# Expert weights kept in SBUF, and expert results scattered into two planes in token order, in a fused attention and mixture-of-experts kernel

## The chip, the cores and the metric

The kernel runs on one core of one Trainium2 chip, in one launch. The time is device microseconds (us) of one execution. A second source is the profile, which is one execution recorded by the hardware profiler: PE is TensorE's matmuls, PEld its weight loads, DVE is VectorE, ACT is ScalarE, POOL is GpSimd, and SP is the engine that only issues transfers. A name such as L1298 is a line of the kernel before.

## What is computed

The input has 8 items (B) of 256 channels and 32 x 32 positions, so 1024 tokens of 256 values each. Everything is float32. Layer 0 is attention with 8 heads of 64, whose softmax runs over the queries, with a projection and a residual. Layer 1 is attention of the normalised tokens with themselves, and then a mixture of 8 experts of which each token uses two:

```python
# layer 0, per item: xt is (S, C)
q, k, v = split(xt @ w_qkv + b_qkv)
attn = softmax(q k^T * SCALE, axis=queries)
t = attn v @ w_out + b_out + xt
# layer 1
a = ln(t); t = t + softmax((a W^T) a^T) a
n = ln(t)
probs = softmax(n @ router_w.T)
rw, re = top_k(probs, 2); rw = rw / rw.sum(-1)
out = n
for e in range(8):
    h = gelu(n @ w1[e] + b1[e])
    out = out + combine[:, e] * (h @ w2[e] + b2[e])
t = t + out        # and back to channels first
```

## The kernel before, in words

The items are worked through in turn. For each item `layer0` runs 32 steps of a head pair g and a key block j: `score` (L493) puts the products of keys and queries into PSUM, two passes on VectorE find the maximum (L508, L517), ScalarE takes the exponential (L534), and `gather_values` (L570) accumulates the result. Then `pr` (L672) projects, and `attend` does the attention of layer 1: `pt` transposes (L281), `px` (L709), score products `ps` in a scheme with seven products (L772), exponentials, transposes of the weights by VectorE, SP transfers and ScalarE copies (`turn`, L861), and eight `mix` steps (`py`, L878; the sum on VectorE at L887). `normed` normalises and turns the result, and `logits` makes the routing scores. In items 0 to 6 `attend` and `normed` call `Begin.at` at named places, and this puts projections and values of the next item (`pqk`, L349, and `pv`, L408) between the steps. In the layer 0 of items 1 to 7, `gather_values` uses empty instructions on SP (`relay.nop()`) to hold an order on TensorE.

The experts are done in two ways. Items 0 to 6 form one group. `dispatch` counts how many tokens go to each expert, gives every choice of a token a row, and scatters normalised tokens into `rows` in DRAM (L1110, two scatters for each of 8 token blocks, from POOL). During layer 0 of item 7, `plan` works out which expert each of 63 blocks of 256 rows belongs to. After layer 0 of item 7, `experts` runs over the 63 blocks in a pipeline written out in its last loop. `fetch` loads a block's rows with four transfers from an address that SP reads from SBUF into a register (L1276, L1281). `weights` has POOL gather 128 rows of 1282 floats, the two weight matrices and both biases, from `wpack` in DRAM (L1264) into one of four buffers `wb`; the gather is skipped by an index out of bounds where the buffer already holds this expert. `turned` transposes on VectorE (L1287), `hidden` multiplies (`ph`, L1298) and applies the gelu on ScalarE (L1308), and `collect` multiplies again (`pe`, L1324), adds the second bias on VectorE (L1334) and has POOL write the block to `y` in DRAM (L1341), in block order. `places` works out meanwhile on VectorE where in `y` each token's two results stand. `wpack` is written at the very start, behind the zero fill of `rows` (L295), by `pack` (L313 to L327).

`Results` then gathers for every block of 128 tokens the two result rows of each token (`yk`, L1420, on POOL), and adds them, times the gate, to the token's sum (L1442, on VectorE). A table of places, `PLACES`, spreads these gathers, adds and stores over the attention of item 7 and over the dense stage. The dense stage, `dense`, does the experts of item 7 without sorting: for each expert and half of the tokens, four products of 512 columns with two weight tiles (`pdh`, L1547), the gelu (L1556), the second product (`pdy`, L1571), and the gated sum (L1580). Its weights come by 16 transfers on SP into three of the `wb` buffers. `store` transposes (L1478) and writes to the output (L1485).

The order on each engine is mostly that of the program, held in places by `tc.issue_after` and `tc.add_manual_dep`.

## Time and profile before

| what | us |
|---|---|
| median of 3 runs (lowest, highest) | 2335.08 (2328.76, 2335.84) |
| profiled execution, its time | 2330.56 |
| profiled execution, span of the core | 2328.6 |
| TensorE busy | 2258.4 (97% of the span) |
| VectorE busy | 1556.0 (67%) |
| ScalarE busy | 1171.3 (50%) |
| GpSimd busy | 409.0 (18%) |
| last `pr` of item 7 to the end of the expert blocks | 1856.9 to 2097.4 |
| attention of item 7, norm and turn | 2097.4 to 2194.4 |
| dense stage | 2194.4 to 2321.3 |

A row of a group gives the line, the engine, the operation, what is written and read with shapes, the count, then busy time and the mean in nanoseconds, and after the second bar the idle time of the engine just before it with what ended it. A row of a stage gives its limits, its length, and for each engine the busy time and the number of instructions, then the granted TensorE clock, the share of time that the 16 DMA engines were busy, and GB/s. A busy TensorE is not a TensorE at its peak; four pairs of a weight load and a matmul of 256 columns follow each other at 1.73 us in the expert stage, though each matmul is listed with 0.38.

### The profile page before, as it was taken

How to read it: one execution, taken by the hardware profiler on the slowest of the kernel's cores; microseconds unless marked ns; L12 is line 12 of the kernel's file. 1: busy time of each engine (PE TensorE's matmuls, PEld its weight loads, DVE VectorE, ACT ScalarE, POOL GpSimd, SP SyncE). 2: the span in 40 equal slices, each digit the busy share in tenths (PEclk: the TensorE clock that was granted, in tenths of full speed). 3: DMA queues.
4: the chain of work that ended last, by engine and by line, in shares of the span. 5: the costliest groups of instructions: out<-in, count | busy, mean ns of one | idle time of the engine just before them, and what ended most of it. 6: DMA issues, size and time to landing. Idle time of an engine off the chain costs nothing.

```text
span 2328.6 us, 37960 instructions
## 1 busy us (share of the span) xinstructions
PE 2258.4 (97%) x13059; PEld 1217.2 (52%) x13059; DVE 1556.0 (67%) x4029; ACT 1171.3 (50%) x2154; POOL 409.0 (18%) x392
## 2 busy tenths in 40 slices
PE   9999999999999999999999999999999999998798
PEld 3344633563456335633564355435553488884565
DVE  5775678557865786578657775777668766436655
ACT  3664466356635663656465647465646622225211
POOL 0000012000200030003000200020002135545553
PEclk9999999999999999999999999999999999999899
DMA  8995201020103010201020101100111156675554
GB/s 293 385 386 153 68 15 42 5 58 10 47 1 63 6 51 1 44 19 53 3 45 19 49 8 28 35 26 13 22 41 42 50 144 191 192 202 141 160 180 136
DMA packets 274407, 199.57 MB, mean 86 GB/s; under 512 B 185224, under 2 KB 227880, under 8 KB 272424
## 3 DMA queue, kind: packets, MB, share of 16 engines
q1 hardware_dynamic: 248120, 138.62, 21.2%
q0 software_dynamic: 25008, 58.01, 7.7%
q8 instruction: 104, 1.70, 0.3%
q10 hardware_dynamic: 1088, 0.52, 0.1%
q14 instruction: 87, 0.71, 0.1%
HBM read 108.88 MB, written 110.90 MB: 94 GB/s over the span
## 4 chain that ended last, share of the span: by engine, by line
PE 81%; ACT 5%; DVE 4%; DMA 3%; issue 3%; SPq 2%; POOL 1%; another core or an unknown queue 1%; DVEq 0%; ACTq 0%; POOLq 0%
PE po L570 19%; PE psc L493 19%; PE pqk L371 7%; PE py L878 6%; PE pr L672 5%; PE pv L408 4%; PE ph L1298 3%; PE pe L1324 3%; PE ps L772 3%; PE pdh L1547 2%; PE pdy L1571 2%; PE px L709 2%; PE pqk L349 2%; SPq L861 2%; PE ps1z L772 1%
## 5 line engine op out<-in xcount | busy, mean ns | idle before, releaser
L534 ACT ACTIVATE ex<-psc,nmax 128x1024 f32<-128x1024 f32 x512 | 570.0, 1114 | 300.1 <-DVE scrap L517 217.9
L493 PE MATMUL psc<-qk,qk 64*64 64x512 f32 x4096 | 575.9, 592 | 3.9 <-ACT ex L534 3.6
L570 PE MATMUL po<-ex,vs 64*64 64x512 f32 x4096 | 570.7, 591 | 3.6 <-DVE vs L550 2.6
L517 DVE TENSOR_SCALAR_CACHE_REDUCE scrap<-psc,nmax 128x512 f32<-128x512 f32 x512 | 384.5, 751 | 159.9 <-PE psc L493 131.9
L508 DVE TENSOR_REDUCE nmax<-psc 128x1 f32<-128x512 f32 x512 | 350.5, 685 | 9.3 <-PE psc L493 9.3
L493 PEld LDWEIGHTS psc<-qk,qk 64*64 64x64 f32 x4096 | 180.4, 132 | 279.3 <-ACT ex L534 132.8
L570 PEld LDWEIGHTS po<-ex,vs 64*64 64x64 f32 x4096 | 176.5, 132 | 275.5 <-DVE vs L550 82.2
L1110 POOL DMA_INDIRECT rows<-n,d_at x112 | 109.0, 973 | 661.2 <-DVE nmax L508 660.9
L1037 POOL TENSOR_TENSOR t<-t,n 128x2048 f32<-128x2048 f32 x8 | 36.3, 4534 | 875.3 <-DVE n L263 875.3
L371 PE MATMUL pqk<-xT,wqkv 128*128 128x512 f32 x384 | 171.2, 599 | 0.0
L336 ACT ACTIVATE qk<-pqk,b_qks 128x512 f32<-128x512 f32 x124 | 85.6, 690 | 86.6 <-PE pqk L371 77.5
L878 PE MATMUL py<-n,spare 128*128 128x256 f32 x512 | 120.2, 391 | 5.1 <-DMA out_dram<-oT 3.3
L1420 POOL DMA_INDIRECT yk<-y,yat x112 | 109.7, 979 | 79.5 <-issue 28.8
L408 PE MATMUL pv<-wqkv,xT 128*128 128x512 f32 x256 | 121.4, 599 | 2.2 <-ACT wqkv L120 1.2
L371 PEld LDWEIGHTS pqk<-xT,wqkv 128*128 128x128 f32 x384 | 71.0, 190 | 99.9 <-issue 76.8
L861 ACT COPY spare<-home 32x256 f32<-32x256 f32 x272 | 109.4, 402 | 15.5 <-DVE home L849 10.5
L878 PEld LDWEIGHTS py<-n,spare 128*128 128x128 f32 x512 | 99.3, 196 | 28.2 <-issue 11.6
L672 PE MATMUL pr<-wo,res 128*128 128x256 f32 x512 | 111.9, 379 | 0.7 <-ACT res L589 0.7
L672 PEld LDWEIGHTS pr<-wo,res 128*128 128x128 f32 x512 | 97.2, 190 | 17.7 <-ACT res L589 4.7
L1308 ACT ACTIVATE hb<-ph,wb 128x256 f32<-128x256 f32 x96 | 40.1, 470 | 127.4 <-issue 86.6
L534 ACT ACTIVATION_READ_ACCUMULATOR ex<-psc,nmax 128x1 f32 x512 | 99.1, 194 | 0.0
L887 DVE SCALAR_TENSOR_TENSOR t<-py,rs,t 128x256 f32<-128x256 f32 x64 | 30.5, 477 | 98.4 <-PE py L878 85.9
(256 smaller groups left out, 2943.3 us busy)
## 6 DMA issues: line engine op xcount, KB each, us to landing
rows<-wb SPq DMA_DIRECT2D x7, 8192.0 KB
xr<-rows SPq DMA_DIRECT2D x252, 64.0 KB
y<-yb POOLq DMA_DIRECT2D x63, 256.0 KB
xs<-in_x_dram SPq DMA_DIRECT2D x64, 128.0 KB
spare<-home SPq DMA_DIRECT2D x240, 32.0 KB
out_dram<-oT SPq DMA_DIRECT2D x60, 128.0 KB
xT<-in_x_dram SPq DMA_DIRECT2D x7, 1024.0 KB
sums<-t SPq DMA_DIRECT2D x7, 1024.0 KB
```

Of the source, the lines that this page charges most:

```text
L371: mm = nc.tensor.matmul(pq[:, ts(n, 512)], wqkv[:, cc, t, ts(g, P)], xT[:, cc, ts(n, 512)], start=(cc == 0), stop=(cc == NCC - 1),)
L408: nc.tensor.matmul(pv, self.xT[:, cc, ts(i, P)], wqkv[:, cc, 2, :], start=(cc == 0), stop=(cc == NCC - 1),)
L493: mm = nc.tensor.matmul(pss[at, h][ts(c, DK), ts(n, 512)], k[r, j * P + c * DK : j * P + (c + 1) * DK], q[r, ts(n, 512)], start=True, stop ...
L508: firsts[at, h] = nc.vector.tensor_reduce(nmax, pss[at, h][:, ts(0, 512)], AX.X, ALU.max, negate=True)
L517: seconds[h] = nc.vector.tensor_scalar(scrap, pss[at, h][:, ts(1, 512)], -1.0, nmaxes[at, h], ALU.mult, ALU.min, accum_out=nmax,)
L534: nc.scalar.activation(ex, pss.pop((at, h)), AF.Exp, bias=nmaxes.pop((at, h)), scale=1.0, accum_out=sums[at][:, h : h + 1],)
L570: mm = nc.tensor.matmul(po[n][ts(h, DK), :], vss[at][keys, h, :], exps[at, h][keys, ts(n, 512)], start=(j == 0 and turn == 0), stop=(j == ...
L672: nc.tensor.matmul(pr[:, :C], res[:, g, ts(i, P)], wo[:, g, :], start=(g == 0), stop=(g == NPAIR - 1))
L861: move(to[ts(k, SQ), a], since[ts(a, SQ), k])
L878: evicted["mixed"] = nc.tensor.matmul(py[:, :D], aT[m], n1[:, m, :], start=(m == 0), stop=(m == NT - 1))
L1110: scatter = nc.gpsimd.indirect_dma_start(out=view[:, :], out_offset=bass.IndirectOffsetOnAxis(ap=ats[k][:, i : i + 1], axis=0), in_=n2[:, ...
L1420: ins = nc.gpsimd.indirect_dma_start(out=self.slot(at)[:, k, :], out_offset=None, in_=self.group.y[:, :], in_offset=bass.IndirectOffsetOnAxis(
```

## The change

At the start of item 7, `keep_experts` loads both weight matrices of all 8 experts into one tile in SBUF, 32 KB in each partition; `pack`, `wpack` and the `wb` buffers go. In the expert stage ScalarE copies the 1024 columns of a block's expert out of the table into a ring of four buffers (`stage`), from an address in a register. The addresses are read from SBUF into registers in lists of 16 blocks: for SP (the rows), ScalarE (weights, and first bias) and VectorE (second bias). The skipping of blocks that share an expert goes: each block has its copy.

Each row of `rows` has two values more, the gate and the place of its result (counted from the end, so that zero means none); POOL writes them beside the normalised tokens before each set of scatters. In `experts` they come by a fifth transfer. `collect` multiplies by the gate, converts the place to an integer, and POOL scatters the 256 result rows by two indirect transfers into `y`, which now has two planes in token order. `places` goes. The products of the last four blocks are put later: `fill` calls their second products in `attend` ("between", "between 2") and in "norm 2", and the first products of the last two at "last weights".

`Results` begins only after item 7 is normed. It loads half items with three direct transfers (the sum and two planes) into five slots, adds twice and stores, one half item at each of the dense steps. `dense` reads weights straight from the table. Since the table has its channels in the order of the 32 x 32 transposes, item 7's norm writes its channels in that order (`squares=True`), the routing uses a router matrix in that order (`rTs`), and the sum of t and n on POOL becomes four instructions. Some tiles change places (layer 0's `res` of item 7, `mixes`).

```diff
-    WROW = NCC * FF + NFC * D + NFC + D
-    NWB = 3
-    NXB = NWB + 1
+    WE = NCC * FF + NFC * D
+    WAYS = 16
+    NXB = 4
+    LATE = 4
+    DW = D + 2
...
+    def keep_experts():
+        table = one.tile([P, E, WE], F32, tag="res", name="table")
+        src = w1.rearrange("e (k cc c) f -> k cc c e f", k=NQ, c=SQ)
+        for k in range(NQ):
+            for cc in range(NCC):
+                nc.sync.dma_start(table[ts(k, SQ), :, ts(cc, FF)], src[k, cc])
+        at = NCC * FF
+        for fc in range(NFC):
+            nc.sync.dma_start(
+                table[:, :, at + fc * D : at + (fc + 1) * D],
+                w2.rearrange("e (fc p) d -> fc p e d", p=P)[fc],
+            )
+        return table
...
-    def pack():
...
+            self.rows = dram.tile([E * self.cap + BR, DW], F32, name=f"rows_{n}")
-            self.y = dram.tile([self.nb * BR, D], F32, name=f"y_{n}")
+            self.y = dram.tile([2 * self.cap, D], F32, name=f"y_{n}")
+            self.planes = self.y.rearrange("(k n p i) d -> n p k i d", k=2, p=P, i=NT)
...
         for k in range(2):
             for i in range(NT):
                 behind = yield
-                view = group.views[2 * (NT * group.items.index(b) + i) + k]
+                if i == 0:
+                    nc.gpsimd.tensor_copy(n2[:, :, D], gate[:, k, :])
+                    nc.gpsimd.iota(
+                        n2[:, :, D + 1],
+                        [[-1, NT]],
+                        base=2 * group.cap - (k * len(group.items) + which) * S,
+                        channel_multiplier=-NT,
...
-    def places(group):
...
+        def register(b, which):
+            if (b, which) not in held:
+                some = min(WAYS, group.nb - b)
+                engine, top = KINDS[which]
+                _, values = nc.values_load_multi_w_load_instructions(
+                    group.where[which][0:1, b : b + some],
+                    engines=[engine],
...
+            return held[b, which]
+
+        ring = one.tile([P, NXB, WE], F32, tag="v", name="w_ring")
+        spare = two.tile([P, LATE // 2, WE], F32, tag="xT", name="w_late")
...
+        def stage(b):
+            late = b - (group.nb - LATE // 2)
+            wb = ring[:, b % NXB] if late < 0 else spare[:, late]
+            firsts[b], seconds[b] = wb[:, :W1], wb[:, W1:]
+            some = W1 if -LATE // 2 <= late < 0 else WE
+            nc.scalar.copy(wb[:, :some], flat[:, bass.ds(register(b, 1), some)])
...
-        def weights(b):
-            wb = wbs_x[b % NXB]
-            nc.gpsimd.indirect_dma_start(
...
+            loads.append(
+                nc.sync.dma_start(
+                    where, group.rows[bass.ds(at, BR), D:].rearrange("(r p) c -> p r c", r=R)
+                )
+            )
...
-                    bias=wb[:, at + fc : at + fc + 1],
+                    bias=b1T[:, bass.ds(at + fc, 1)],
...
-                    wb[:, at : at + D].unsqueeze(1).to_broadcast([P, R, D]),
-                )
+                    b2_flat[:, bass.ds(register(b, 3), D)].unsqueeze(1).to_broadcast([P, R, D]),
+                )
+                where = wheres.pop(b)
+                nc.vector.tensor_mul(yb, yb, where[:, :, 0:1].to_broadcast([P, R, D]))
+                to = small.tile([P, R], I32, tag="to", name=f"to_{n}_{b}", bufs=4)
+                nc.vector.tensor_scalar(
+                    to, where[:, :, 1], -1.0, float(2 * group.cap), ALU.mult, ALU.add
+                )
-            nc.gpsimd.dma_start(group.y[ts(b, BR), :].rearrange("(r p) d -> p r d", r=R), yb)
+            for r in range(R):
+                nc.gpsimd.indirect_dma_start(
+                    out=group.ways[R * b + r][:, :],
+                    out_offset=bass.IndirectOffsetOnAxis(ap=to[:, r : r + 1], axis=0),
+                    in_=yb[:, r, :],
...
         for b in range(group.nb + 4):
-            if b - 3 in rows:
+            if b - 3 in rows and b - 3 < group.nb - LATE // 2:
                 hiddens[b - 3], last = hidden(b - 3, rows.pop(b - 3))
+            if 0 <= b - 1 < group.nb:
+                stage(b - 1)
             if b < group.nb:
                 rows[b] = fetch(b)
...
     class Results:
-        SLOTS = 8
-        PLACES = {
...
+            self.sent += 1
+            nc.sync.dma_start(self.totals[at], self.group.sums[n][:, ts(h, NB), :])
             for k in range(2):
+                nc.sync.dma_start(
+                    self.slots[at][:, k], self.group.planes[n][:, k, ts(h, NB), :]
+                )
...
+        def add(self, behind):
...
+            with tc.issue_after(behind.ins):
+                for k in range(2):
+                    nc.vector.tensor_add(total, total, self.slots[at][:, k])
...
+        def tick(self, k, behind):
+            if self.stored < self.added:
+                self.store()
+            if self.added < len(self.todo):
+                self.add(behind)
...
-            if n == NH2 - 1 and e + NWB < E:
-                weights(e + NWB)
...
+        if b == B - 1:
+            table = keep_experts()
...
-        experts(groups[0], evicted["divided"])
-        others = Results(groups[0])
-        others.begin()
+        product, result = experts(groups[0], evicted["divided"], table)
...
+            if place == "between":
+                result(end - 4)
+            elif place == "between 2":
+                result(end - 3)
+            elif place == "last weights":
+                product(end - 2)
+                product(end - 1)
+            elif place == "norm 2":
+                with tc.issue_after(evicted["mixed"].ins):
+                    result(end - 2)
+                    result(end - 1)
```

## The prediction

> **What bounds the kernel now.** I read the busy row by slice first, then busy time by stage, then waits, then the chain that ended last.
>
> ```profile
> PE   9999999999999999999999999999999999998798
> PEclk9999999999999999999999999999999999999899
> POOL 0000012000200030003000200020002135545553
> ```
> TensorE is full, and in full clock, until the last tenth. Only the end, where GpSimd is busy too, has holes. Stages, with PE, PEld, DVE, ACT, POOL, clock, DMA share, GB/s:
>
> ```profile
> 1870.75:2097.40 226.65, 220.78 (x1009) 190.22 (x1008) 112.30 (x291) 54.16 (x128) 107.66 (x120) 1.00 0.67 185
> 2099.76:2181.55 81.79, 68.81 (x216) 42.84 (x216) 52.02 (x119) 41.64 (x91) 46.91 (x48) 0.92 0.60 162
> 2181.55:2194.35 12.80, 4.98 (x25) 2.85 (x24) 11.66 (x30) 0.41 (x2) 6.37 (x5) 0.83 0.74 218
> 2194.35:2321.30 126.95, 120.75 (x422) 77.82 (x418) 72.64 (x170) 24.30 (x37) 60.88 (x61) 0.96 0.49 146
> 1635.15:1702.84 67.69, 64.93 (x225) 40.43 (x224) 35.79 (x85) 41.43 (x91) 0.00 (x0) 1.00 0.23 39
> ```
> They are: the expert blocks; item 7's attention from px to its last mix; from there to the dense stage; the dense stage; and, last, item 6's attention over the same steps as item 7's. Item 6 needs 14.1 us less although it also does two value products (3.4 us) for an item that follows: its VectorE has 16 us less to do, and its clock is 1.00 against 0.92. So item 7's attention is held up by the gathering and adding put into it.
>
> ```profile
> L1442 DVE SCALAR_TENSOR_TENSOR o<-yk,gate,o 128x256 f32<-128x256 f32 x44 | 18.4, 476 | 0.0
> L1420 POOL DMA_INDIRECT yk<-y,yat x52 | 50.7, 975 | 36.3 <-issue 12.5 <-DVE t L887 10.7 <-DVE o L1442 5.0
> PE ph L1298 <- DMA wb<-wpack,w_at: 4.5, 6, 1.2
> PE py L878 <- DMA out_dram<-oT: 3.3, 1, 3.3
> ```
> The first two rows cover that attention stage; the last two are waits of TensorE. In the expert stage the chain itself leaves TensorE again and again for a y store and then weights, here at 1914 us (start, us, what).
>
> ```profile
> 1914.06 4.22 DMA y<-yb
> 1918.29 2.90 issue
> 1921.18 5.71 DMA wb<-wpack,w_at
> 1927.03 1.97 PE ph L1298 x8
> ```
>
> **The change, part by part.** The sum is against the profiled execution (2330.56 us, span 2328.6); the median of the runs, 2335.08, is 4.5 above it, and I carry the difference over to the median.
>
> *Start.* Packing the weights goes (SP busy with it 153 to 212 us, after the zero fill). In item 0 the steps px to last mix take 72.6 us (189.50 to 262.14), in item 1 66.8 (435.59 to 502.36): 5.8 us lost while this traffic drains. The fill stays, with rows 0.8% longer. Taken: -4.5; ends -6 and +2 (odd row lengths might write slower; no row shows it).
>
> *Expert stage.* A block is 1.727 us for ph and 1.727 for pe; 63 make 217.6, the stage takes 226.65, so stalls are 9. Four pe and two ph halves, 6 x 1.727 = 10.4, move to later. What stays: 120 x 1.727 + 0.4 at the start = 207.6, or -19.0 before new waits. The new work per 3.45 us block:
> - ACT: gelus 0.84 a pair, plus a copy of 128x1024. Nearest rows: exp over 128x1024 in SBUF 1.15, 128x512 copy 0.585, 32x256 copy 0.402, so 0.95 to 1.15; I take 1.1. With address arithmetic (SP's own, 0.05 to 0.15) about 2.2: covered by the wait for ph.
> - DVE: transpose 0.70, add 0.69, the new gate product (same shape) 0.69, the index conversion 0.15: 2.2. The `places` work goes. Covered.
> - POOL: two indirect scatters at 0.97 to 1.03 (rows of the scatters and of the weight gathers) against 1.03 + 0.77 now: 2.1, covered. yb has two buffers, 6.9 us; 1.5 (DVE) + 2.1 + some 2.5 to land is 6.1. If landing takes 4.2, as the chain shows with weights in the way, DVE waits 1 us, and the two PSUM buffers hide it.
> - SP: a fifth DMA per block, 256 short pieces, 0.32 to 0.65: 2.7 of 3.45; fetches run 3 blocks ahead.
> - Register loads, in lists of 16: ACT two lists, DVE and SP one, every 16 blocks. This is the one part that nothing covers. The row:
>
> ```profile
> L1276 SPq TENSOR_LOAD <-row_at x63: 263/276/1116, 1856.3 to 2074.8; - x63
> ```
> At 0.276 a list is 4.4 us in which its engine starts nothing else. Behind the list of weight addresses stands the copy for block 16 (ready at 7.3 us, PE wants it at 6.9: 0.4 late); behind that of the bias addresses stands the gelu of block 16, 1.2 late, for which pe waits; behind DVE's stands the next xb transpose, 1.2 late. That is 2.8 us, three times, and some 2 at the start, where the first bias list may sit behind item 7's square root at 1872.8. Together 10. The Trainium skill ("DMA: Bandwidth & Descriptors", Latency and other measured facts) speaks against the change: a floor of about 0.6 us per `tensor_load`. A list is then 9.6 us, copy and gelu are 5.6 and 7.2 late, 38 for three groups, with start and DVE 44 to 55: an estimate, and the whole gain. I go by the row, whose 63 loads are of the same kind on another engine. Ends: 2 (lists hoisted or overlapped) and 55. Taken: -19.0 + 10 = -9.0.
>
> *Item 7's attention.* Gathers, 44 adds, five transposes for stores and the weight loads leave. Item 6 is the model: 67.7, less its own filling (3.4), plus two pe and two ph halves (6.9) = 71.2, against 81.8: -10.6. Ends -14 and 0: the results bring DVE 1.5 us each, and two gelu pairs bring ACT 1.7 plus a table load of 1.28 and perhaps one back. Cover is the slack that item 6 shows; if it is gone, each comes whole.
>
> *Last mix to dense.* Now 12.8: the norm of seven blocks runs after adds and transposes on DVE. Then: the norm of the last block 2.5, beside two pe halves (3.45); DVE work on their results 3.0, then nT copies of 1.22 each, 8.7 together: -4.1. The add of t and n on POOL becomes four instructions with 32-element runs, 4.5 to 9 us (now 4.53 in one), behind two result scatters: done 14 to 17 us after the last mix; the first dense add wants it at 19.
>
> *Dense.* TensorE's own work is 16 x 6.88 + some 7.5 for routing and biases = 117.6; the stage takes 126.95. The rest, 9.4, lies at 2211 to 2226, 2261 and 2284 to 2290, where DVE stands at adds whose gathered rows are late and TensorE's sums stand behind them; most of it goes with the gathers. The DVE load per step is then 4 x 0.477 + two adds of 128x1024 (1.22 each by the copy of that shape) + transpose 1.24 = 5.6 of 6.88. Transfers per step are 1.57 MB loaded in 4 KB pieces and 0.52 MB stored in 512 B pieces. Rates:
>
> ```profile
> 2.00:5.00 3.00, 3.00 (x4) 1.05 (x4) 0.00 (x0) 0.10 (x1) 2.99 (x17) 1.00 0.94 351
> 1694.00:1700.00 6.00, 5.10 (x24) 4.21 (x23) 0.89 (x2) 0.58 (x1) 0.00 (x0) 1.00 0.85 164
> ```
> 351/0.94 = 373 GB/s for long pieces, 164/0.85 = 193 for 512 B pieces: 4.2 + 2.7 = 6.9 us, just the step. Five slots hold four steps (27 us) of lead, the first lands some 16 us after the last mix and is wanted at 21, so it is hidden. Taken: -6; ends -8 and +10.
>
> *Elsewhere.* Scatter rows of 1032 B, two small POOL instructions per set and a few plan operations of 0.2: nothing, behind item layers in which POOL is idle; without that cover under 3. The table's 4 MB goes out on SP at item 7's start; TensorE's first value products come 10 us later; if they waited behind ten issues of 0.5, 5 us.
>
> Sum: -4.5 - 9.0 - 10.6 - 4.1 - 6 = -34.2: 2335.1 - 34.2 = 2301.
>
> **Rivals.** (1) *Attention does not recover*: the fills land on its chain, so -10.6 and -4.1 shrink to nothing: 2316. For: DVE and ACT get new work there. Against: item 6 carries comparable fills. (2) *Dense becomes transfer bound*: with rates a quarter lower a step takes 9.3 us (5.7 + 3.6); 14 loads and the nine stores before the last of them are 112 us, from 12 after the last mix, when the scattered rows have landed, to 124; the last add wants them at 108. 16 more: 2317. For: 6.9 against 6.88. (3) *Slower, by register loads on ACT*: place and price as above. Without any load stall the sum is -44; from about 0.6 us per value it is used up, and at 1.1 (the largest of the row) copy and gelu are 13.6 and 15.6 late, 88 for three groups and some 20 at the start: +64, 2399. For: the rule, and the row's maximum. Against: the median.
>
> **How the numbers follow.** My forecast 0.55 (2301, its own range 2284 to 2316); rival 1 0.17, rival 2 0.13, rival 3 0.10, mixtures that end near nothing 0.05. No change means within 0.3%, 2328 to 2342, about what a measurement here can tell. Faster 0.83, the same 0.06, slower 0.11. The range begins at 2281 (favourable ends, a little cut) and goes up to 2328, leaving out no change, slower and 3% below.
>
> **What would show it.** Right: no chain step through wb in the expert stage, ph and pe at 1.73 except near blocks 16, 32 and 48; py back to 0.38 us and clock 1.00 in item 7's attention; no gather rows; dense steps of 6.88. Wrong: TensorE waiting for ACT's copies or gelu throughout the expert stage; long TENSOR_LOADs on ACT; DVE adds of dense waiting for planes; item 0 unchanged.

## The result, and the profile after

The changed kernel takes 2308.87 us (median of 4 runs, 2307.36 to 2309.37) where the kernel before took 2332.12 (4 runs, 2328.76 to 2335.84): a ratio of 0.9899, 95% interval 0.9879 to 0.9919, or 23 us less. The forecast was 34 us less, 2301. Repeated on a second chip (in the experiments) it was 2309.70 against 2328.14, ratio 0.9922 (0.9908 to 0.9936): 18 us less. The profiled span is 2307.6 us both times.

The busy rows by slice, from the page of the changed kernel:

```profile
PE   9999999999999999999999999999999989999996
PEclk9999999999999999999999999999999999999998
POOL 1000012000200030003000200021001225551100
```

Two holes stand out in TensorE, where before there were several: slice 33, at the start of the experts, and the last slice. POOL is done two slices earlier than TensorE; the gathers of results are gone. The stages, with PE, PEld, DVE, ACT, POOL, granted clock, DMA share and GB/s; in this order item 0 from px to its last mix, the experts from their first ph to pt, item 7's attention from px to its last mix, from there to the dense stage, the dense stage until TensorE's last matmul, and what follows it:

```profile
190.33:257.10 66.77, 64.92 (x226) 40.71 (x225) 35.86 (x86) 41.42 (x91) 0.00 (x0) 1.00 0.44 105
1869.77:2083.89 214.12, 209.67 (x961) 183.14 (x960) 124.94 (x252) 114.72 (x183) 113.87 (x116) 0.99 0.59 139
2086.34:2157.20 70.86, 68.83 (x249) 45.08 (x250) 39.12 (x94) 44.60 (x97) 3.91 (x4) 1.00 0.26 66
2157.20:2164.16 6.96, 5.75 (x41) 4.59 (x40) 6.08 (x15) 0.20 (x1) 2.76 (x2) 1.00 0.00 0
2164.16:2286.50 122.34, 119.79 (x422) 78.19 (x418) 80.59 (x131) 24.33 (x37) 6.50 (x7) 0.97 0.64 202
2286.50:2307.60 21.10, 0.00 (x0) 0.00 (x0) 10.49 (x10) 0.00 (x0) 0.00 (x0) 0.56 0.61 149
```

The last row is the news: 21 us in which TensorE does nothing. Against the profile of before:

| stage | before | changed | difference | forecast |
|---|---|---|---|---|
| item 0, px to last mix | 72.6 | 66.8 | -5.8 | -4.5 |
| end of that to item 7's pr | 1594.7 | 1597.1 | +2.4 | 0 |
| pr and experts, to pt | 240.6 | 229.7 | -10.9 | -9.0 |
| item 7's attention | 81.8 | 70.9 | -10.9 | -10.6 |
| last mix to dense | 12.8 | 7.0 | -5.8 | -4.1 |
| dense, to the last matmul | 126.95 | 122.34 | -4.6 | -6 |
| after the last matmul | 7.3 | 21.1 | +13.8 | no term |

With 0.8 of later start in item 0 the differences add up to the 21 us between the two spans. Six stages came within 2.5 us of the forecast, each for itself; the seventh took back 14. The second pair of profiles gives the same picture with another split: item 0 -4.5, from there to item 7's pr +2.9, experts -13.1, attention -12.8, last mix to dense -6.1, dense -0.4, after the last matmul +13.8.

What fills the last 21 us is in VectorE's timeline of the changed kernel (start us, us, engine, line, operation, count, and in brackets what the engine waited for just before):

```profile
2287.30 1.24 DVE L1474 STREAM_TRANSPOSE oT<-total 128x1024 f32<-128x1024 f32 x1
2288.46 2.44 DVE L1456 TENSOR_TENSOR total<-total,ys_v 128x1024 f32<-128x1024 f32 x2
2290.82 1.24 DVE L1474 STREAM_TRANSPOSE oT<-total 128x1024 f32<-128x1024 f32 x1
2292.36 1.25 DVE L1474 STREAM_TRANSPOSE oT<-total 128x1024 f32<-128x1024 f32 x1 [0.30 <-DMA out_dram<-oT]
2296.03 1.25 DVE L1474 STREAM_TRANSPOSE oT<-total 128x1024 f32<-128x1024 f32 x1 [2.42 <-DMA out_dram<-oT]
2298.04 1.25 DVE L1474 STREAM_TRANSPOSE oT<-t 128x1024 f32<-128x1024 f32 x1 [0.77 <-DMA out_dram<-oT]
2301.36 1.25 DVE L1474 STREAM_TRANSPOSE oT<-t 128x1024 f32<-128x1024 f32 x1 [2.08 <-DMA out_dram<-oT]
```

Six halves are still to be transposed and stored when TensorE ends: four of other items (oT from total) and the two of item 7 (oT from t). There are two oT buffers, so each transpose soon waits for the store of the one before the last: the last four follow each other at 3.0 us, though each takes 1.25. So the stores set the pace of what is left, but not how much is left. In mid-dense VectorE waited for no plane load and no store: these six were simply behind in its order.

The register lists, which the forecast gave 10 us and its slower rival over 100, are here (ns min/median/max, first and last start):

```profile
L1273 ACTq TENSOR_LOAD <-w_at x4: 1018/1122/1454, 1848.0 to 1976.5; - x4
L1273 ACTq TENSOR_LOAD <-b_at x4: 1020/1026/1657, 1870.1 to 2040.3; - x4
```

A list of 16 costs about 1.1 us, not 16 times 0.276. From the third block on ph and pe follow each other at 1.727 us, through blocks 16, 32 and 48 as well; the one exception is a wait of 0.43 us shortly before the end. What the experts do lose, they lose at their start (TensorE):

```profile
1854.17 15.77 PE L689 MATMUL pr<-wo,res 128*128 128x256 f32 x64 [1.98 <-ACT res L606]
1869.77 1.89 PE L1332 MATMUL ph<-xb,w_ring 128*128 128x256 f32 x8
1872.05 1.99 PE L1332 MATMUL ph<-xb,w_ring 128*128 128x256 f32 x8 [0.39 <-DVE xb L1321]
1873.88 1.97 PE L1359 MATMUL pe<-w_ring,hb 128*128 128x256 f32 x8
1879.48 3.58 PE L1332 MATMUL ph<-xb,w_ring 128*128 128x256 f32 x8 [3.63 <-DVE xb L1321]
```

and why, on ScalarE:

```profile
1849.75 3.88 ACT L1294 COPY w_ring<-table 128x1024 f32 x4 [0.56 <-DVE vs L567]
1853.54 1.06 ACT L606 COPY res<-po 128x512 f32<-128x512 f32 x2
1870.03 1.99 ACT L1294 COPY w_late<-table 128x1024 f32 x2 [15.43 <-PE pr L689]
1872.04 1.28 ACT L1343 ACT_TABLE_LOAD   x1
1873.33 0.84 ACT L1343 ACTIVATE hb<-ph,b1T 128x256 f32<-128x256 f32 x2
1874.19 1.28 ACT L280 ACT_TABLE_LOAD   x1
1875.48 0.21 ACT L280 ACTIVATE rstd_a<-rstd_a 128x8 f32<-128x8 f32 x1
```

Four ring copies stand ahead of the res copies that pr wants. Then two copies for the very last blocks and a Gelu stand ahead of the square root of item 7's norm; VectorE waits for that root (3.73 us at 1875.72) before it can go on to the transposes xb.

The waits cost more than their length. The eight ph records behind the wait of 3.63 us (the four products of a half block, each recorded as two) take 3.58 us instead of 1.89; the granted clock from 1879.48 to 1882.90 was 0.52. The 64 records of pr behind the wait of 1.98 take 15.77 instead of 14.08, at 0.89.

### The profile page after: what moved, and what is told of

The parts are those of the page before. It is cut to its first block, busy times and chain, and to the rows that moved or that the text cites. A ratio compares the mean times of both kernels' runs of the same rounds, so it can differ in the third digit from the quotient of the medians.

```text
span 2307.6 us, 38039 instructions
## 1 busy us (share of the span) xinstructions
PE 2248.4 (97%) x13061; PEld 1213.5 (53%) x13061; DVE 1567.6 (68%) x3922; ACT 1238.8 (54%) x2221; POOL 313.6 (14%) x313
## 4 chain that ended last, share of the span: by engine, by line
PE 83%; DVE 5%; ACT 5%; SPq 4%; issue 2%; DMA 1%; POOL 0%; DVEq 0%; ACTq 0%; POOLq 0%
PE po L587 19%; PE psc L510 19%; PE pqk L380 7%; PE py L897 7%; PE pr L689 5%; PE pv L417 4%; PE ph L1332 3%; PE ps L791 3%; PE pe L1359 3%; PE pdy L1547 2%; PE px L728 2%; PE pdh L1524 2%; SPq L880 2%; PE pqk L358 2%; PE ps1z L791 2%
## 5 line engine op out<-in xcount | busy, mean ns | idle before, releaser
L551 ACT ACTIVATE ex<-psc,nmax 128x1024 f32<-128x1024 f32 x512 | 570.0, 1114 | 301.4 <-DVE scrap L534 218.5
L1380 POOL DMA_INDIRECT y<-yb,to x126 | 123.6, 981 | 191.7 <-DVE yb L1374 165.4
L1332 PE MATMUL ph<-xb,w_ring 128*128 128x256 f32 x488 | 117.2, 384 | 4.5 <-DVE xb L1321 4.5
L897 PE MATMUL py<-n,spare 128*128 128x256 f32 x512 | 114.9, 379 | 0.0
L1359 PE MATMUL pe<-w_ring,hb 128*128 128x256 f32 x472 | 111.6, 379 | 0.0
L1332 PEld LDWEIGHTS ph<-xb,w_ring 128*128 128x128 f32 x488 | 93.6, 192 | 18.5 <-DVE xb L1321 5.7
```

Source lines behind the costliest of these rows:

```text
L551: nc.scalar.activation(ex, pss.pop((at, h)), AF.Exp, bias=nmaxes.pop((at, h)), scale=1.0, accum_out=sums[at][:, h : h + 1],)
L897: evicted["mixed"] = nc.tensor.matmul(py[:, :D], aT[m], n1[:, m, :], start=(m == 0), stop=(m == NT - 1))
L1332: last = nc.tensor.matmul(ph[:, ts(fc, BR)], wb[:, dc * FF + fc * P : dc * FF + (fc + 1) * P], xb[:, dc, :], start=(dc == 0), stop=(dc == ...
L1359: mm = nc.tensor.matmul(py[:, ts(r, D)], hT[:, fc, ts(r, P)], wb[:, ts(fc, D)], start=(fc == 0), stop=(fc == NFC - 1),)
```

## The experiments

My theory after the two profiles: the miss is VectorE's order in the dense stage (the 21 us at the end), and what the experts lose is ScalarE's and VectorE's order at their start. The rivals: transfers bound the tail; the first fetches or register lists bound the start. The later experiments ask whether the forecast's own terms (register loads, fills, packing) were what they were taken for. Stages are read from each profile as in the table above. The first four experiments ran on one chip, the changed kernel's repetition and the two after it on a second, the next three on a third, the last on a fourth. The changed kernel itself was timed only on the chip of the result and on the second of these, and the kernel before differs between chips: on the chip of the first four experiments it takes 2316.68 us (10 runs), 15 less than where the result was taken. So a total of an experiment is compared with the changed kernel only where both ran on one chip, and read by stages elsewhere. A stage that an edit leaves alone repeats well: item 0 takes 66.7 to 66.8 us in every profile of the changed kernel and its variants but the last, on four chips.

**The order of VectorE in the dense stage.** Each step's L1556 may only come behind the adds and the transpose handed out by the steps before:

```
-                    nc.vector.tensor_add(total, total, self.slots[at][:, k])
+                    self.done = nc.vector.tensor_add(total, total, self.slots[at][:, k])
...
-            store(self.group.items[n], self.totals[at], h)
+            self.kept = store(self.group.items[n], self.totals[at], h)
...
+                    with (
+                        tc.issue_after(others.done.ins) if others.done else nullcontext(),
+                        tc.issue_after(others.kept.ins) if others.kept else nullcontext(),
+                    ):
                         added = nc.vector.scalar_tensor_tensor(
```

> The changed kernel with one thing altered: in the dense tail each collect's additions on VectorE (L1556) may only be issued behind the adds (L1456) and the transpose (L1474) that the step before them has handed out. Nothing is added or removed. Theory A, the order fixed when the kernel is built: in the changed kernel these adds and transposes slip behind the L1556 of the following step, one more place every few steps, so that six transposes with their stores are left when TensorE ends (21.2 us). In order, only the two of item 7 are left, as in the kernel before (7.3 us): tail 7 to 9 us, dense matmuls still 6.88 us a step, total 12 to 14 us below the changed kernel, about 2296. Rival B, the transfers set it (two oT buffers, each half's store some 3.5 us, plane loads in the same queue): then the transposes forced into their places wait for 'DMA out_dram<-oT' or for the plane loads in mid-dense, the L1556 behind them wait too, TensorE's steps grow past 6.88 us, and the total moves by less than 4 us.

Measured: 2299.57 us (5 runs, 2299.41 to 2300.63), span 2297.8. Its stage rows for dense and what follows:

```profile
2163.17:2288.30 125.13, 118.78 (x422) 77.32 (x418) 87.38 (x137) 24.31 (x37) 6.47 (x7) 0.99 0.68 212
2288.30:2297.80 9.50, 0.03 (x1) 0.00 (x0) 3.18 (x4) 0.00 (x0) 0.00 (x0) 0.77 0.57 144
```

The tail is 9.5 instead of 21.1, as theory A had it but for half a microsecond. Theory A's dense steps of 6.88 throughout did not come: dense took back 2.8, and by the stages the gain is 9 us and not the 12 to 14 expected. The last steps of TensorE show the reason:

```profile
2269.80 3.62 PE L1549 MATMUL pdy<-table,dh 128*128 128x256 f32 x16
2274.46 3.69 PE L1549 MATMUL pdy<-table,dh 128*128 128x256 f32 x16 [1.05 <-DVE t L1562]
2279.55 3.69 PE L1549 MATMUL pdy<-table,dh 128*128 128x256 f32 x16 [1.39 <-ACT dh L1535]
2284.63 3.69 PE L1549 MATMUL pdy<-table,dh 128*128 128x256 f32 x16 [1.40 <-DVE t L1562]
```

In this stage the order is not the program's: the kernel's builder had put the hidden products of these steps ahead, so four sums stood together, the last of them at VectorE's pace of 5.09 us. So the 21 us came of the order of one engine: the transfers were the same, and nobody waited for them in mid-dense. Why the builder lets the adds slip (its estimate of the loads is the natural suspect) was not tried.

**The order at the start of the experts.** Item 7's norm is handed over before the experts, the ring copies come behind the res copies, the two late copies behind the newest Gelu:

```
+        n1 = one.tile([P, NT, D], F32, tag="n", name=f"n1_{b}")
+        layer_norm(t1, n1, 1e-5, f"a{b}")
         product, result = experts(groups[0], evicted["divided"], table)
...
+            with tc.issue_after((gelus[-1] if late >= 0 else evicted["copied"]).ins):
                 nc.scalar.copy(wb[:, :some], flat[:, bass.ds(register(b, 1), some)])
```

> The changed kernel with only the start of the expert blocks altered: ScalarE issues the two res copies (L606) ahead of the four ring copies (L1294), the two w_late copies late instead of in front of the first Gelu, and item 7's layer norm is handed to the scheduler ahead of the experts, so that its Sqrt comes before the first Gelu table. Theory A: the 6.7 us by which the first stretch of the experts is slower than its steady pace (pr waits 1.3 for res copies, pr paced 15.8 instead of 14.1, ph waits 3.6 and 0.4 for the transposed rows) are ScalarE's and VectorE's order: pr to the last expert matmul 229.7 becomes 223 to 225, total 4 to 7 us below the changed kernel, 2302 to 2305. Rival B: the first row fetches (DMA) or the first register lists set the start, and it stays within 2 us. A miss of another kind: the late copies meet the Gelus near the end and give part of it back there.

Measured: 2300.62 us (5 runs, 2300.39 to 2302.06), span 2299.2. From pr to pt 222.6 us instead of 229.7 (228.6 in the experiment above, which ran on the same chip with this part unchanged: 6.0 less by that comparison). TensorE:

```profile
1852.83 14.08 PE L690 MATMUL pr<-wo,res 128*128 128x256 f32 x64 [0.68 <-ACT res L606]
1866.74 1.89 PE L1335 MATMUL ph<-xb,w_ring 128*128 128x256 f32 x8
1869.57 1.97 PE L1335 MATMUL ph<-xb,w_ring 128*128 128x256 f32 x8 [0.93 <-DVE xb L1324]
1871.37 1.89 PE L1362 MATMUL pe<-w_ring,hb 128*128 128x256 f32 x8
1873.09 1.89 PE L1335 MATMUL ph<-xb,w_ring 128*128 128x256 f32 x8
```

The wait for res is back to the 0.68 of the kernel before, the wait of 3.63 is gone and one of 0.93 is left. Theory A holds, a little beyond its upper end; the three moves were made together, and their shares were not measured apart. The slow pace goes with the waits: the ph half behind the 0.93 takes 1.97 us, at a granted clock of 1.00. All eight profiles with the changed kernel's start (the two of the changed kernel, and the experiments that leave this part alone) have the wait of 3.6 to 3.7 us, and behind it ph at a clock of 0.50 to 0.52. For pr the link is looser: with the wait of 1.98 ahead of it, it takes 15.77 us at 0.89 in four of the eight and 14.08 at 1.00 in the other four (among them the experiment above, and the changed kernel on its second chip); with the wait of 0.68 it takes 14.08 in all six profiles, the kernel before's two among them. So this order permits the 1.7 us of pr but does not decide it; what does is open.

**POOL's order.** The last result scatters ahead of the four t+n adds:

```
+          with tc.issue_after(evicted["scattered"].ins):
             for part, at in ((n2.first, ...), (n2.last, ...)):
                 ... nc.gpsimd.tensor_add(some, some, part...)
```

> The changed kernel with POOL's last result scatters (L1380) put ahead of its four t+n adds (L1066). Theory A: the multiplication L1374 of 2.58 us beside the POOL add goes back to about 0.69 and the wait of 0.76 for POOL goes, so n2T's second copy is ready some 2.5 us earlier and the second half of pl/pdh no longer waits 2.53 us; the plane loads may also start some 4 us earlier. Total 2 to 3.5 us below the changed kernel. Rival B: the copies of n2T then stand beside the POOL adds and are stretched themselves, or the adds hold back the first L1556; total within 1 us. If the tail after TensorE's end is bound by the order of VectorE alone, the earlier plane loads do nothing to its 21 us.

Measured: 2311.17 us (6 runs, 2307.53 to 2313.10), span 2311.3; dense is 124.2 where the changed kernel's two profiles have 122.3 and 123.7: no gain. The first half of the story came true, in that pl's second half no longer waits 2.53 us. Then the same collision came back at another place. VectorE's timeline of the changed kernel, then VectorE's and POOL's of this run:

```profile
2163.45 2.58 DVE L1374 TENSOR_TENSOR yb<-yb,where 128x512 f32<-128x512 f32 x1
2168.53 0.68 DVE L1374 TENSOR_TENSOR yb<-yb,where 128x512 f32<-128x512 f32 x1
```
```profile
2173.49 0.22 DVE L1010 TENSOR_TENSOR g_hot<-g_p,g_top 128x64 f32<-128x64 f32 x1
2173.75 5.22 DVE L1011 TENSOR_TENSOR g_hot<-g_hot,rank 128x64 f32<-128x64 f32 x1
```
```profile
2174.33 4.15 POOL L1067 TENSOR_TENSOR t<-t,n 128x896 f32<-128x896 f32 x2
2178.41 0.88 POOL L1067 TENSOR_TENSOR t<-t,n_last 128x128 f32<-128x128 f32 x2
```

A product of 64 columns took 5.22 us instead of 0.22: it ended as the third of the four POOL adds did (2178.9). The gates were late, and the bias products waited 0.91 and 1.36 us. In the changed kernel the same adds had met the product L1374 (2.58 instead of 0.68). The Trainium skill ("SBUF — State Buffer", Who interferes with whom) says that a VectorE instruction with two inputs in SBUF contends with a POOL instruction that reads SBUF. Here both rows agree with that, and moving the adds only chose the victim. That a product which began 0.6 us ahead of the adds was held over three of them is what this trace adds.

**The three orders together**, the edits being those of the three experiments above.

> The three orders together (dense tail, start of the experts, POOL's scatters). If the three causes are the ones named and lie in different stages, the gains add: 13 + 6 + 3 = 22 us below the changed kernel, about 2287, 45 below the kernel before. If the transfers bound the tail, what is won ahead of the dense stage is lost in it again, and the sum is below 12.

Measured: 2295.11 us (4 runs, 2292.88 to 2296.02), span 2293.8; 222.3 from pr to pt, dense 127.7, tail 9.4. Against the first profile of the changed kernel that is 7.4 us less at the experts and 11.7 in the tail, less the 5.4 that dense now takes back: 14 by the spans, and the third order is no gain. The expected 22 was too much by what dense takes back and by the third. If the transfers bound the tail, nothing of the first two would have added.

**The changed kernel and the kernel before on another chip.**

> The changed kernel itself, unaltered, beside the kernel before on the chip of this comparison, since the kernel before was 0.7% faster on the chip of the first experiments than where the change was timed. Theory A: the gain belongs to the stages (item 0's pack, the experts, the attention's fill, less the tail) and stands: 20 to 23 us below the kernel before. Rival B: part of it is what the pack's transfers cost on one chip and not on another: then 8 to 15 us below. The second stretch of the profile that should not change between chips is the 21 us after TensorE's end.

> The kernel before itself, for its profile on this chip. If the stages of it that wait for transfers (item 0 from px to its last mix, 72.6 us; the attention of item 7, 81.8 us; the dense stage, 127 us) differ from those of the profile already shown, the difference of the two chips lies in the transfers or in the granted clock; each stage's granted clock says which.

Measured: 2309.70 us (5 runs, 2308.50 to 2311.42), the kernel before 2328.14 (17 runs). So the gain is 18 us here and 23 on the first chip, with the tail at 21.1 both times. The kernel before has medians from 2316.7 to 2334.6 on the five chips of this study, the changed kernel 2308.9 and 2309.7 on the two where it ran. By stages, this chip's profile of the kernel before differs from the first one by 1.5 us less in item 0, 1.3 more in the experts, 1.8 more in the attention and 2.8 less in dense; no one stage explains it. On a chip where the kernel before takes 2316.7 the change is worth less. How much less was not timed; an estimate for the chip of the first four experiments, from the first one's profile up to pt (2082.9) and the second one's from pt on (223.7), is a span of 2306.6 for the changed kernel and a time of some 2308.4, about 8 us below the kernel before there. Why that one is faster on such a chip is open: no profile of it was taken there.

**One register to a load.**

```
-    WAYS = 16
+    WAYS = 1
```

> The changed kernel with every register loaded by its own instruction (WAYS 1 instead of 16): 63 loads of each of the four kinds in the place of 4. Theory A: a load costs what it costs whatever it fetches, about 1.1 us as a list of 16 does now. Then ScalarE has 1.9 us of copies and Gelus and 2 x 1.1 of loads in a block of 3.45, 4.1 us, and the experts' stage grows by 0.6 us a block or more, 40 us and up; lists are what makes the loads free. Rival B: a single load costs 0.28 us, as the forecast's row for single loads had it, 2.5 us a block, and the time stays within 3 us of the changed kernel.

Measured: 2308.50 us (4 runs, 2304.58 to 2311.99), the same as the changed kernel on that chip. The loads:

```profile
L1273 ACTq TENSOR_LOAD <-w_at x63: 272/278/484, 1848.0 to 2071.3; - x63
L1273 DVEq TENSOR_LOAD <-b_at x63: 300/533/682, 1877.3 to 2162.1; - x63
```

A single load costs ScalarE 0.278 us; two of them, a copy of 1.04 and a pair of Gelus of 0.84 are 2.4 us in a block of 3.45. Theory B holds: neither as lists nor one by one do the loads cost anything here.

**Two orders, without the third**: the edits of the first two experiments.

> The changed kernel with the two orders that helped, the dense tail's on VectorE and the start of the experts on ScalarE, without the scatters put ahead of the POOL adds. If that third order cost the 2 us that its own profile shows (a gate multiplication of 5.22 us beside the POOL adds, the biases late), this is 1 to 3 us below the three together: about 2292 to 2294 where those gave 2295.

Measured: 2293.74 us (4 runs, 2291.51 to 2295.21), span 2291.8, ratio to the kernel before on that chip 0.9852 (0.9835 to 0.9868). That is 16 us below the changed kernel on the same chip.

**TensorE's order in the dense stage as well.** Hidden products of a step only behind the sums of the step two before it:

```
+                  with tc.issue_after(sums[-1].ins) if sums else nullcontext():
                     nc.tensor.matmul(ph[:, ts(fc, 512)], ...)
...
+            sums.append(mm)
             others.tick(e * NH2 + n, added)
```

> The version with two orders, and in the dense stage TensorE's order fixed as well: the hidden products of a step (pdh) may only be issued behind the sums (pdy) of the step two before it. In the version with two orders the builder had put pdh ahead, so that the last four pdy stood together, each 5.09 us (VectorE's four L1556, two adds and a transpose: 1.6 + 2.5 + 1.2) instead of 3.45 of TensorE's own, with waits of 1.0 to 1.9 for VectorE. Theory A: with steps of 6.88 throughout, VectorE's 5.3 us hide again, the dense matmuls end 3 to 5 us earlier, total 2289 to 2291. Rival B: the builder had put them ahead because plane loads or stores are late there; then VectorE's forced order waits for transfers, TensorE waits for VectorE in mid-dense instead, and the total stays within 1.5 us of 2293.7.

Measured: 2292.75 us (5 runs, 2290.35 to 2294.24), span 2290.9, ratio 0.9813 (0.9797 to 0.9829) on a chip where the kernel before takes 2334.6. The stage rows of dense, of the version with two orders and of this one:

```profile
2155.61:2282.50 126.89, 120.46 (x422) 78.26 (x418) 87.45 (x138) 24.31 (x37) 6.51 (x7) 0.97 0.67 209
```
```profile
2157.84:2281.60 123.76, 119.76 (x422) 78.26 (x418) 88.06 (x138) 24.32 (x37) 6.51 (x7) 0.97 0.68 214
```

Dense is 3.1 us shorter, its steps are 6.88 from the third on, and VectorE waits for no transfer. The total gained only 1, because the stages ahead of dense ended 2.2 us later on this chip; the program of those does not differ between the two kernels. Inconclusive as a total, clear as a stage. Its median is the lowest of the study.

**The late blocks before the attention.** Nothing is filled into item 7's attention:

```
+        result(end - 4)
+        result(end - 3)
+        product(end - 2)
+        product(end - 1)
+        result(end - 2)
+        result(end - 1)
...
         def fill(place):
-            if place == "between":
-                result(end - 4)
...
```

> The changed kernel with nothing put into item 7's attention: the last blocks' six halves (two ph, four pe) are computed at the end of the expert stage. The output is the same. Theory A, the attention has holes of its own that these halves fill: the expert stage grows by 10.4 us (6 x 1.727), the attention from px to its last mix falls from 70.7 to about 64 (item 6's 67.7 less its own filling of 3.4), the way from the last mix to the dense stage stays or falls by under 2, sum +2 to +5. Rival B: the halves cost the attention their full time; then attention and the way to dense fall by 10 us together and the total does not move. That the attention is 70.7 without gathers and 81.8 with them would be the same in both.

Measured: 2316.66 us (4 runs, 2310.40 to 2319.57), span 2312.2. Of the profile, attention and experts:

```profile
2098.83:2168.30 69.47, 63.53 (x216) 39.72 (x216) 35.38 (x86) 41.63 (x92) 2.23 (x2) 0.98 0.34 88
1867.94:2096.02 228.08, 221.55 (x1010) 192.80 (x1008) 130.63 (x262) 118.28 (x191) 120.55 (x122) 0.99 0.58 134
```

The experts grew by 14.0 (10.4 of work; TensorE also waits 1.50 and 0.63 us for the late weights' copies and a Gelu), the attention fell by 1.4 only. Dense fell by 3.0 and what follows it by 3.3: five halves are left there instead of six, and no scatter comes after the last mix; which did how much was not tried. The sum, +5 by the spans, is theory A's upper end, but the split is neither theory's, and the total does not settle it: the changed kernel was not timed on this chip, and against the kernel before this version has a ratio of 0.9917 (0.9893 to 0.9940), between the changed kernel's 0.9899 and 0.9922. By the stages: by itself the attention takes 69.5 us and not 64, at a granted clock of 0.98. TensorE is idle for 6 us of it, and the four fills that otherwise lie there (two ph and two pe halves, 6.9 us) cost it 1.4.

**The packing's traffic.** First, eight transfers of w1 behind the zero fill and ahead of the next item's x:

```
         nc.sync.dma_start(group.y[:P, :], zero[:, :D])
+        wp = dram.tile([E * P, NCC * FF], F32, name="wpack")...
+        for k in range(NQ):
+            for cc in range(NCC):
+                nc.sync.dma_start(wp[:, ts(k, SQ), ts(cc, FF)], src[k, cc])
```

> The changed kernel with a part of the removed packing put back as mere traffic: eight transfers of w1 from DRAM to DRAM (2 MB) behind the zero fill, into a buffer that nobody reads. Nothing else waits for them. Theory A, the traffic is what item 0 lost in the kernel before: its transfers run on to about 220 us instead of 202, and item 0 from px to its last mix takes 71 to 73 us instead of 66.7, total +4 to +6. Rival B, what item 0 lost was the order of the engines' work and ScalarE's waits, not the traffic: 66 to 68 us and no change in the total.

Measured: 2353.67 us (4 runs, 2352.57 to 2355.95). This answered another question:

```profile
225.14 5.87 PE L363 MATMUL pqk<-xT,wqkv 128*128 128x512 f32 x8 [42.37 <-DMA xT<-in_x_dram]
```

TensorE waited 42 us for the next item's x, which stood behind the added transfers on SP. Afterwards item 0's stage took its 66.8. So six of them were put behind that load, with every other engine's order untouched:

> The changed kernel with six transfers of w1 from DRAM to DRAM (1.5 MB) behind the next item's x in SP's queue, into a buffer that nobody reads: in the run before, they stood ahead of that load and TensorE waited 42 us for it, which says nothing of the traffic. Every engine's order of work is that of the changed kernel. Theory A, traffic alone is what item 0 lost in the kernel before: transfers run on to some 225 us, beside the first shuffles aT<-home at 213 and 220, and item 0 from px to its last mix takes 70 to 73 us instead of 66.7; total +3 to +6, 2312 to 2316. Rival B, the shuffles have room enough and the loss was the order in which the builder put the engines' work around the pack: 66.5 to 67.5 us, total within 1.5 us of the changed kernel.

Measured: 2314.46 us (21 runs, 2310.98 to 2318.62), 5 above the changed kernel where that ran, on other chips; the kernel before takes 2316.76 on this one. The stage row of item 0, px to last mix, and the shuffles of this run and of the kernel before:

```profile
190.08:263.50 73.42, 66.65 (x226) 41.96 (x225) 36.10 (x85) 41.43 (x91) 0.00 (x0) 0.95 0.62 166
```
```profile
L888 SPq DMA_DIRECT2D aT<-home x8: 585/618/1782, 218.5 to 226.6; - x8
```
```profile
L861 SPq DMA_DIRECT2D aT<-home x8: 585/608/688, 212.2 to 217.2; - x8
```

It is 6.7 us more than without them, what the kernel before lost (5.8). The way is not quite the same: here the shuffles aT were issued at 218.5 instead of 213.0, since SP was busy with the transfers until 217; in the kernel before they were issued at 212.2 and VectorE then waited 6.4 us for the sums that use them. So it is shown that transfers put in front of the shuffles can cost item 0 some 6 us; it is not shown that the kernel before lost its 5.8 in the same way, since its shuffles were issued in time. How much of this is SP's time, how much the landing and how much the order of the work around the packing is not separated.

## Why the prediction was right or wrong, point by point

- *Start, -4.5*: item 0 fell by 5.8 and 4.5 in the two pairs. Right in size. The traffic experiment gives a cost of this size back, but by shuffles issued 5.5 us late, which the kernel before did not have, so the cause as forecast is likely and not shown. The filling itself did become slower, not by 0.8% but from 386 to some 350 GB/s, and ended some 20 us later; nothing in item 0 needed the queue before 213 us, so that was free.
- *Expert stage, -9.0*: measured -10.9 and -13.1, with the wrong parts. The term "register lists, 10" is nothing: a list takes 1.1 us and no step of TensorE is late for it. In its place stand 6 to 7 us of stalls at the start which the forecast had not: ScalarE's new copies ahead of res and of the norm's root, VectorE behind that root, and TensorE at half its clock after the wait. I had named item 7's square root there, but as the thing that a list would stand behind. Without these stalls the stage is -18, where the forecast's sum without list stalls was -19.
- *Rival 3, slower by register loads*: false. The rule that I weighed against the row, the floor of about 0.6 us per `tensor_load` (the Trainium skill, "DMA: Bandwidth & Descriptors", Latency and other measured facts), does not hold for ScalarE and SP here: 0.278 and 0.273 us singly. VectorE's single loads, at 0.533, come near it. For a list both rule and row were multiplied by 16, and that was the mistake: it is one instruction. (The lateness given there to the gelu, 7.2 and 15.6 us, does not follow from the 1.2 by the length of the list, which would make it 6.4 and 14.4; nothing rests on it now.)
- *Item 7's attention, -10.6*: 70.9 against a forecast of 71.2. Right in size, and the granted clock is back to 1.00 as forecast, but the model held two errors that cancelled: item 6's time without its fills (64) was taken for item 7's own, which is 69.5, and the fills were given their full 6.9 where they cost 1.4 by the experiment. That the sum came out within 0.3 us was luck.
- *Last mix to dense, -4.1*: -5.8. The POOL adds came ahead of the scatters and not behind them as I wrote; the product L1374 beside them was stretched, and the loss appears after the start of dense, as 2.53 us before pl's second half.
- *Dense, -6*: -4.6 and -0.4. Steps of 6.88 and no wait for planes, as forecast; so rival 2, the transfer bound, is false.
- *The step that failed* is the last sentence of that part, "Five slots hold four steps (27 us) of lead ... so it is hidden". It followed the transfers and VectorE's load per step (5.6 of 6.88), and both were right. It never asked in which order VectorE would take the adds, the transposes and the sums. They slipped behind, and 13.8 us of stores came out after TensorE's end, where nothing covers them. That is the whole of the miss, 11 us by the medians and 13 by the spans: the other stages of the table together gave 35.6, 1.4 more than forecast.
- *Rival 1* is false: both its stages recovered.

The time lies inside the range, 8 us above the forecast's 2301. Part of that nearness is luck: list stalls of 10 us that do not exist stood where 6 to 7 us of unforeseen stalls came, and two errors in the attention offset each other. The mechanism was right in the main (weights from SBUF end the waits for gathers, and the attention recovers), and what it left out is the tail. Putting VectorE's order right alone gives 2299.6, on another chip. The range's lower end, 2281, is not what the favourable ends of the parts add up to: -49, which is 2286.

## What to carry to other kernels

When work is moved to the end of a kernel, load per step and bandwidth per step say only that it could be hidden; look also at the order in which the one engine that does it will issue it, and count how many pieces are left when the bounding engine ends. An engine that is given new early work (here ScalarE's copies) delays whatever was next in its order, so list the first ten instructions of each engine after the change, not only its load. Before an order is changed to end a collision of VectorE with POOL, see which VectorE instructions with two SBUF inputs lie at the new place.

## What the runs showed of the hardware

- One TENSOR_LOAD that fetches 16 values takes 1.0 to 1.7 us on ScalarE; one that fetches a single value takes 0.278 us there and 0.533 on VectorE. Per value a list is four times cheaper.
- A VectorE product of 128x64 lasted 5.22 us instead of 0.22 beside four POOL adds of 2.1, 2.1, 0.5 and 0.5 us, and ended as the third of them did.
- Behind a wait of 3.6 to 3.7 us of TensorE its granted clock was 0.50 to 0.52 for the next 3.4 to 3.6 us, in all eight profiles that have this wait; behind one of 0.93 at the same place it was 1.00. Behind a wait of 1.98 us ahead of pr it was 0.89 over pr in four profiles and 1.00 in four others with the same instructions.
- The zero fill with rows of 1032 bytes ran at 331 to 357 GB/s, with rows of 1024 bytes at 385 to 386.
